# One plan for the orders of all engines in the second stage of a four-layer GNN kernel, and Strassen's scheme for one LSTM step

## The chip, the cores and the metric

The kernel runs on one core of a Trainium2 chip, in one launch, all in fp32. The metric is the device time of a run in microseconds (us). TensorE is called PE, VectorE DVE, ScalarE ACT, GpSimd POOL, and SyncE, which issues DMAs, SP.

## What is computed

The input x has 128 graphs of 64 nodes with 256 features; all share one 64 x 64 adjacency matrix. Four layers follow, each `x = layernorm(x + layer(x))`:

```
layer 0   three graph convolutions with adj * adj: 256 -> 512 -> 1024 -> 256, relu after the first two
layer 1   eigenvectors U of the normalised Laplacian: U (relu(U^T x W1 + b1) W2 + b2)
layer 2   two graph convolutions with adj (256 -> 256), then, for p = 1, 2, 3, 4:
          an LSTM of p steps over each window of p nodes; its last hidden state replaces the window's last node
layer 3   h = x W + b; softmax over nodes of (h h^T * adj), times h
```

One LSTM step has eight units of 128 outputs, four gates (i, f, g, o) in two halves of the hidden size:

```python
g = x_t @ Wih.T + h @ Whh.T + bias
i, f, gg, o = jnp.split(g, 4, axis=-1)
c = sigmoid(f) * c + sigmoid(i) * tanh(gg)
h = sigmoid(o) * tanh(c)
```

## The kernel before

**Tiles and stages.** The 8192 rows are 64 tiles of 128 rows (two graphs), taken as 16 groups of four tiles. All rows lie in SBUF in X for the whole run. The first stage does layer 0 for all groups (`layer0`, L744), its middle product already by Strassen's scheme (L777 to L840), while `eigen` finds U on DVE in small steps in between. The norms of the first stage are ACT and POOL steps kept in a list, `norms`; each product of `layer0` takes one off (L832). What is left of the list is done in the second stage. Layers 1 to 3 are the second stage: `group` (L1187) is a generator through `layer1`, `layer2` with `lstm`, and `layer3`.

**Matmuls.** `mm` (L715) issues one matmul and moves a planner's clock, `now`. Nearly all matmuls of the kernel are put down to its line 716; transposes go through `turn` (L925, line 926).

**LSTM.** `hT` holds the group's features on partitions, 64 nodes x 8 graphs on the free axis. `lstm(hT, p, first, nw)` (L991) runs p steps over nw windows, so matmuls have n = 8 nw columns: 256 for p = 1 and 2, 168 for p = 3, 128 for p = 4. In a step t > 0, each of the eight units has four matmuls into one PSUM bank, two with `wih` (from x) and two with `whh` (from h, L1029), then a tanh on ACT with the bias from PSUM (L1030). Sigmoids are taken as tanh of half the argument. DVE then forms c (L1034 to L1038), ACT its tanh (L1039), DVE the new h (L1041, or L1051 into `hT`). The first two units' `wih` matmuls go ahead of the wait for h (L1008).

**What sets the order.** PE's order in the second stage is written out by hand, under `manual_schedule` for PE alone (L1205). Three groups (WAYS) are under way. A generator yields the time at which its next step may start: the clock plus a fixed allowance (MOVE, MIXED, LIN, CONV, NORM, SOFT and CELL, L922 and L923, 1.2 to 5.2 us). The loop takes the oldest group whose time has come (L1214); once no group is left to start, the one with the fewest steps done, with LEAD = 10 steps of advance for each older group. DVE, ACT and POOL aren't under `manual_schedule`: the framework orders their instructions, with two copies given priority (L952, L1122). The last two groups (ENDING) do layer 3 in two halves and their last norms on ACT.

**Engines and waits.** Every engine takes its instructions in order and waits on semaphores. A group's step passes from PE through PSUM (eight banks) to ACT or DVE and back to PE.

Of the kernel before, what the change touches and what calls it, by code (L numbers as in the profile page):

```python
# [1 line left out]

# [8 lines left out]
F32 = mybir.dt.float32  # L11
# [4 lines left out]
N = 64  # L16
# [24 lines left out]
class Timed:  # L41
# [6 lines left out]
    def __getattr__(self, name):  # L48
        def give(out, *args, **kw):
            self.free[0] = max(self.free[0], self.until[0]) + self.least + 0.0009 * max(0, np.prod(out.shape[1:]) - 64)  # L50
            return getattr(self.engine, name)(out, *args, **kw)  # L51

        return give

# [484 lines left out]
LEAD = 10  # L539
# [57 lines left out]
def kernel(  # L597
# [51 lines left out]
    X = keep.tile([P, NT, D], F32, name="X")  # L649
# [4 lines left out]
    nc.scalar.dma_start(X[:, 2:4, :], x_t[:, 2:4, :])  # L654
    for t in range(2):
        nc.sync.dma_start(X[:, t, :], x_t[:, t, :])
# [6 lines left out]
    for t in range(4, NT, 2):  # L663
        nc.sync.dma_start(X[:, t:t + 2, :], x_t[:, t:t + 2, :])
# [79 lines left out]
    def layer0(g):  # L744
        xs = X[:, 4 * g:4 * g + 4, :]
# [108 lines left out]
        for t in (2, 0):  # L854
            p = tl(psa, [P, 2, D], "ps", bufs=6)
            mm(p, sqT2, s3[:, t:t + 2, :])
            yield now[0]
            x2 = xs[:, t:t + 2, :]
            VL.tensor_add(x2, p, x2)
            norms.extend(scalar_norm(tc, small, x2, half, spare))  # L860

# [45 lines left out]
    pg = ctx.enter_context(tc.tile_pool(name="pg", bufs=WAYS, reuse_waits="tile"))  # L907
    pw = ctx.enter_context(tc.tile_pool(name="pw", bufs=5, reuse_waits="tile"))
    pv = ctx.enter_context(tc.tile_pool(name="pv", bufs=4, reuse_waits="tile"))
    psb = ctx.enter_context(tc.tile_pool(name="psb", bufs=8, space=bass.MemoryType.PSUM, reuse_waits="tile"))  # L910
# [10 lines left out]
    now[0] = due[0] = 0.0  # L921
    MOVE, MIXED, LIN, CONV, NORM, SOFT = 1.2, 1.2, 1.5, 1.8, 5.2, 5.2  # L922
    CELL = {256: 3.8, 168: 2.2, 128: 1.9}  # L923

    def turn(out, in_):  # L925
        PE.transpose(out, in_, ident)  # L926
        now[0] += 0.11

    def work():
        return tl(pw, [P, 1024], "w")  # L930

    def work2():
        return tl(pv, [P, 512], "v")

    spare[0] = lambda: work2()[:, :D]

    def ps4(shape=(P, 512)):
        return tl(psb, list(shape), "ps")
# [4 lines left out]
    def mixed(src, rhs, ready):  # L943
# [3 lines left out]
        for t in range(4):  # L947
            if t % 2 == 0:
                yield ready[t // 2]
            for c in range(2):  # L950
                mm(ps[c][:, t * P:(t + 1) * P], src[:, t, c * P:(c + 1) * P], rhs)
        with tc.high_priority(offset=1500):  # L952
            V.tensor_copy(dst[:, 0, :], ps[0])
        S.copy(dst[:, 1, :], ps[1])
        yield now[0] + MIXED
        return dst

    def norm(xs, t, ready, more=0.0, scalar=False):
        rows_norm(tc, small, xs[:, t:t + 2, :], half, scalar)
        ready.append(now[0] + NORM + more + (0.8 if ready else 0.0))  # L960

    def layer1(xs, ready):
        a = yield from mixed(xs, u2, ready)
        for t in range(0, 4, 2):
            V.tensor_add(xs[:, t:t + 2, :], xs[:, t:t + 2, :], ub2.unsqueeze(1).to_broadcast([P, 2, D]))
        h = as3(work2(), 4)
        for t in range(0, 4, 2):
# [5 lines left out]
            yield now[0]  # L973
        yield now[0] + LIN
        z = work2()
        p = ps4((P, 4, P))
        for t in range(4):
            mm(p[:, t, :], h[:, t, :], ut2)
        S.copy(as3(z, 4), p)
        yield now[0] + MOVE  # L980
        ready = []
        for t in range(0, 4, 2):
            p = ps4((P, 2, D))
            for j in range(2):
                mm(p[:, j, :], z[:, (t + j) * P:(t + j + 1) * P], bw2)
            V.tensor_add(xs[:, t:t + 2, :], p, xs[:, t:t + 2, :])  # L986
            norm(xs, t, ready, 2.0)
            yield now[0]
        return ready

    def lstm(hT, p, first, nw):  # L991
# [6 lines left out]
        for t in range(p):  # L998
# [4 lines left out]
            G = tl(pg, [P, 2048], "gates")[:, :2 * len(names) * n].rearrange("p (q h n) -> p q h n", h=2, n=n)  # L1003
            gate = {q: G[:, i] for i, q in enumerate(names)}
            units = [(h, q) for h in range(2) for q in names]

            ahead = {}
            early = units[:2] if t else []  # L1008
            for h, q in early:
                m = slice(("ifgo".index(q) * 2 + h) * P, ("ifgo".index(q) * 2 + h + 1) * P)  # L1010
                ahead[h, q] = pp = ps4()[:, :n]
                for k in range(2):
                    mm(pp, wi[:, k, m], xt[k], k == 0, False)
            if t:
                yield ready
            if p > 1 and not t:
                c = tl(pg, [P, 512], "c")[:, :2 * n].rearrange("p (h n) -> p h n", h=2)
            new = None if last else tl(pg, [P, 512], "hs")[:, :2 * n].rearrange("p (h n) -> p h n", h=2)
            for h, q in units:
                j = 2 * "ifgo".index(q) + h  # L1020
                m = slice(j * P, (j + 1) * P)
                pp = ahead.get((h, q))
                if pp is None:
                    pp = ps4()[:, :n]
                    for k in range(2):
                        mm(pp, wi[:, k, m], xt[k], k == 0, k == 1 and not t)
                if t:
                    for k in range(2):
                        mm(pp, wh[:, k, m], hs[:, k, :], False, k == 1)  # L1029
                S.activation(gate[q][:, h, :], pp, AF.Tanh, bias=bias[:, j:j + 1], scale=0.5 if q == "g" else 0.25)  # L1030
                if q == "g":
                    to = gate["g"][:, h, :] if t or p == 1 else c[:, h, :]
                    if t:
                        V.scalar_tensor_tensor(c[:, h, :], gate["f"][:, h, :], 1.0, c[:, h, :], op0=ALU.add,  # L1034
                                               op1=ALU.mult)
                    V.scalar_tensor_tensor(to, gate["i"][:, h, :], 1.0, gate["g"][:, h, :], op0=ALU.add, op1=ALU.mult)  # L1036
                    if t:
                        V.scalar_tensor_tensor(c[:, h, :], c[:, h, :], 0.5, to, op0=ALU.mult, op1=ALU.add)  # L1038
                    S.activation(gate["i"][:, h, :], c[:, h, :] if p > 1 else to, AF.Tanh, scale=0.5)  # L1039
                if q == "o" and not last:  # L1040
                    V.scalar_tensor_tensor(new[:, h, :], gate["o"][:, h, :], 1.0, gate["i"][:, h, :], op0=ALU.add,  # L1041
                                           op1=ALU.mult)
                if q == "o":
                    if h == 0:
                        yield now[0]
                elif h == 1 or len(units) == 8:
                    yield now[0]
# [7 lines left out]
            ready = now[0] + CELL[n]  # L1055
            hs = new
        return ready

    def layer2(xs, g, ready):
        a = yield from mixed(xs, adT2, ready)  # L1060
        g1 = as3(work(), 4)
        ready = []
        for t in range(0, 4, 2):
            p = ps4((P, 2, D))
            for j in range(2):
                run(p[:, j, :], [(a[:, k, (t + j) * P:(t + j + 1) * P], cw0[:, k, :]) for k in range(2)])
            V.tensor_add(g1[:, t:t + 2, :], p, wide["c_b0"].unsqueeze(1).to_broadcast([P, 2, D]))
            relu(g1[:, t:t + 2, :], g1[:, t:t + 2, :])
            ready.append(now[0] + CONV)
            yield now[0]  # L1070
        a = yield from mixed(g1, adT2, ready)
        hT = tl(pw, [P, 1024], "w").rearrange("p (k n b) -> p k n b", k=2, b=8)
        for c in range(2):
            p = ps4((P, 4, P))
            run(p, [(cw1[:, k, c * P:(c + 1) * P], a[:, k, :]) for k in range(2)])
            h = work2()
            V.scalar_tensor_tensor(as3(h, 4), rs_row.unsqueeze(1).to_broadcast([P, 4, P]), cb1[:, c:c + 1], p,
                                   op0=ALU.mult, op1=ALU.add)
            S.activation(hT[:, c, :, :].rearrange("p n b -> p b n"), as3(h, 8), AF.Relu, scale=2.0)
            yield now[0]  # L1080
        ready = now[0] + CONV
        for p, first, nw in ((1, 0, 32), (1, 32, 32), (2, 0, 32), (3, 0, 21), (4, 0, 16)):
            if first == 0:
                yield ready
            ready = yield from lstm(hT, p, first, nw)
        hb = as3(work(), 2)
        V.tensor_copy(as3(hb[:, 0, :], 8), hT[:, 0, :, :].rearrange("p n b -> p b n"))
        S.copy(as3(hb[:, 1, :], 8), hT[:, 1, :, :].rearrange("p n b -> p b n"))
        yield ready + 1.6
        ready = []  # L1090
        for t in range(0, 4, 2):
            p = ps4((P, 2, D))
# [169 lines left out]
```

## Time and profile before

| | us |
|---|---|
| median of 3 runs (2534.43 to 2536.97) | 2536.52 |
| the profiled execution | 2540.87 |
| its span, first to last instruction | 2539.1 |
| PE busy | 2494.8 |
| DVE busy | 1407.8 |
| ACT busy | 1090.6 |
| POOL busy | 134.2 |

The profile is of one execution, whose own time is 2540.87 us, 1.8 us more than its span. An engine's busy time is the time in which at least one of its instructions was under way. Matmuls overlap one another and their ends are modelled. PEld is the loading of weights, which overlaps matmuls. A row of the windows view has a stretch and its length in us, then the busy us of PE, PEld, DVE, ACT and POOL with instructions in brackets, the granted PE clock as a share of full speed, the DMA share and GB/s. A row of the waits view has the waiting engine, what it wrote and the line, then what released it: us in total, times, longest. A row of the timeline has start, us from the first start to the last end, engine, line, operation, output<-inputs, shapes and how many in a row.

### The profile page before, as it was taken

The numbers are of one execution on the slowest core, as the hardware profiler recorded it, in microseconds if no ns is written. First come the engines' busy times: TensorE is split into PE (matmuls) and PEld (weight loads), VectorE is DVE, ScalarE is ACT, GpSimd is POOL, SyncE is SP. The second block draws the span as 40 slices with busy tenths as digits, with TensorE's granted clock in tenths as the row PEclk, the third lists the DMA queues.
The fourth block names the chain that finished last, engine by engine and source line by source line (L and its number), as shares of the span: only waits on it lengthen the run. The fifth ranks groups of instructions, "written<-read, shape, count | busy, mean of one in ns | idle before, by whom it ended". The sixth has DMA issues, their size and how long they took to land.

```text
span 2539.1 us, 39015 instructions
## 1 busy us (share of the span) xinstructions
PE 2494.8 (98%) x15020; PEld 2196.2 (86%) x15020; DVE 1407.8 (55%) x4996; ACT 1090.6 (43%) x2706; POOL 134.2 (5%) x316
## 2 busy tenths in 40 slices
PE   9999999999999999999999999999999999999997
PEld 7788887888878889998989889898998998978996
DVE  6888777778885433454453543544445345353235
ACT  2344333433333344445344444444444534535454
POOL 0000000000000100000000000000000000010001
PEclk9999999999999999999999999999999999999998
DMA  6000000000000300000000000000000000000000
GB/s 219 1 1 1 1 1 1 1 1 1 1 1 1 117 1 1 10 9 1 9 9 1 9 1 10 9 1 9 1 9 9 1 9 9 1 9 1 1 1 26
DMA packets 24634, 32.09 MB, mean 13 GB/s; under 512 B 2176, under 2 KB 21376, under 8 KB 24448
## 3 DMA queue, kind: packets, MB, share of 16 engines
q1 hardware_dynamic: 24096, 29.32, 3.4%
q8 instruction: 118, 1.93, 0.3%
q14 instruction: 68, 0.56, 0.1%
q10 hardware_dynamic: 352, 0.28, 0.0%
HBM read 21.20 MB, written 8.39 MB: 12 GB/s over the span
## 4 chain that ended last, share of the span: by engine, by line
PE 91%; DVE 5%; POOL 2%; issue 1%; DMA 0%; ACT 0%; SPq 0%; ACTq 0%; POOLq 0%; DVEq 0%
PE ps L716 88%; PE ps L926 2%; POOL ln_rs L554 1%; DVE X L564 1%; DVE ln_st L551 1%; DVE D L51 1%; PE ps L1146 1%; PE pc L93 1%; DMA X<-in_x_dram 0%; POOL ln_rs L553 0%; DVE tw L51 0%; DVE ln_mv L552 0%; DVE X L1176 0%; DVE X L986 0%; DVE X L1096 0%
## 5 line engine op out<-in xcount | busy, mean ns | idle before, releaser
L716 PE MATMUL ps<-w,wih 128*128 128x256 f32 (+2 forms) x4992 | 894.0, 319 | 1.8 <-DVE w L1051 1.8
L716 PEld LDWEIGHTS ps<-w,wih 128*128 128x128 f32 x4992 | 760.9, 191 | 47.8 <-issue 5.7
L1030 ACT ACTIVATE gates<-ps,cbi 128x128 f32<-128x128 f32 (+2 forms) x1248 | 499.3, 410 | 523.3 <-PE ps L716 516.2
L716 PE MATMUL ps<-hs,whh 128*128 128x128 f32 (+2 forms) x3072 | 540.5, 303 | 6.2 <-DVE hs L1041 6.2
L716 PEld LDWEIGHTS ps<-hs,whh 128*128 128x128 f32 x3072 | 453.9, 191 | 32.9 <-issue 11.2
L1036 DVE SCALAR_TENSOR_TENSOR gates<-gates 128x256 f32<-128x256 f32 (+2 forms) x256 | 89.3, 349 | 297.4 <-ACT gates L1030 297.4
L716 PE MATMUL ps<-aw,h 128*128 128x256 f32 x1024 | 227.2, 379 | 0.0
L716 PEld LDWEIGHTS ps<-aw,h 128*128 128x128 f32 x1024 | 192.9, 190 | 25.9 <-ACT h L725 0.5
L725 ACT ACTIVATE h<-h 128x512 f32<-128x512 f32 x128 | 80.5, 629 | 170.0 <-DVE h L51 169.8
L1039 ACT ACTIVATE gates<-c 128x128 f32<-128x128 f32 (+2 forms) x288 | 98.1, 341 | 114.1 <-DVE c L1038 87.9
L1034 DVE SCALAR_TENSOR_TENSOR c<-gates,c 128x128 f32<-128x128 f32 (+2 forms) x192 | 62.6, 326 | 139.4 <-ACT gates L1030 138.2
L1051 DVE SCALAR_TENSOR_TENSOR w<-gates 128x256 f32<-128x256 f32 (+2 forms) x160 | 59.6, 376 | 108.5 <-PE ps L716 73.5
L716 PE MATMUL ps<-ss,tw 128*128 128x256 f32 x512 | 117.9, 380 | 0.0
L716 PE MATMUL ps<-ss,aw 128*128 128x256 f32 x512 | 117.3, 379 | 0.0
L716 PE MATMUL ps<-m,aw 128*128 128x256 f32 x512 | 117.1, 380 | 0.0
L716 PE MATMUL ps<-aw,m 128*128 128x512 f32 x256 | 114.8, 594 | 0.0
L1041 DVE SCALAR_TENSOR_TENSOR hs<-gates 128x128 f32<-128x128 f32 (+2 forms) x192 | 62.6, 326 | 93.6 <-ACT gates L1039 52.4
L553 POOL TENSOR_SCALAR ln_rs<-ln_mv 128x2 f32<-128x2 f32 x96 | 26.2, 273 | 1558.4 <-DVE ln_mv L552 1557.9
L716 PEld LDWEIGHTS ps<-ss,aw 128*128 128x128 f32 x512 | 96.6, 190 | 12.8
L716 PEld LDWEIGHTS ps<-ss,tw 128*128 128x128 f32 x512 | 96.3, 190 | 12.9 <-issue 0.2
L564 DVE TENSOR_SCALAR X<-X,ln_mv,ln_rs 128x256 f32<-128x256 f32 x176 | 64.7, 410 | 75.9 <-POOL ln_rs L554 75.9
L716 PEld LDWEIGHTS ps<-m,aw 128*128 128x128 f32 x512 | 95.6, 190 | 12.6 <-issue 0.5
(294 smaller groups left out, 3107.4 us busy)
## 6 DMA issues: line engine op xcount, KB each, us to landing
X<-in_x_dram SPq DMA_DIRECT2D x30, 256.0 KB, 6.3
out_dram<-X SPq DMA_DIRECT2D x28, 256.0 KB, 2.1
wih<-in_c_ih_dram SPq DMA_DIRECT2D x4, 1024.0 KB, 7.2
aw<-in_a_w_dram SPq DMA_DIRECT2D x3, 1024.0 KB, 10.3
whh<-in_c_hh_dram SPq DMA_DIRECT2D x3, 1024.0 KB, 9.4
out_dram<-X SPq DMA_DIRECT2D x8, 128.0 KB, 1.7
aw<-in_a_w_dram SPq DMA_DIRECT2D x1, 512.0 KB, 5.8
cw<-in_c_w_dram SPq DMA_DIRECT2D x2, 256.0 KB, 5.1
```

The source lines that it names most:

```text
L51: return getattr(self.engine, name)(out, *args, **kw)
L553: nc.gpsimd.tensor_scalar(rs, mv[:, :, 1], EPS, None, op0=ALU.add)
L564: nc.vector.tensor_scalar(x[:, t, :], x[:, t, :], mv[:, t, 0:1], rs[:, t:t + 1], op0=ALU.subtract, op1=ALU.mult)
L716: PE.matmul(out, lhsT, rhs, start=start, stop=stop)
L725: S.activation(dst, src, AF.Relu)
L926: PE.transpose(out, in_, ident)
L1030: S.activation(gate[q][:, h, :], pp, AF.Tanh, bias=bias[:, j:j + 1], scale=0.5 if q == "g" else 0.25)
L1034: V.scalar_tensor_tensor(c[:, h, :], gate["f"][:, h, :], 1.0, c[:, h, :], op0=ALU.add, op1=ALU.mult)
L1036: V.scalar_tensor_tensor(to, gate["i"][:, h, :], 1.0, gate["g"][:, h, :], op0=ALU.add, op1=ALU.mult)
L1039: S.activation(gate["i"][:, h, :], c[:, h, :] if p > 1 else to, AF.Tanh, scale=0.5)
L1041: V.scalar_tensor_tensor(new[:, h, :], gate["o"][:, h, :], 1.0, gate["i"][:, h, :], op0=ALU.add, op1=ALU.mult)
L1051: V.scalar_tensor_tensor(hT[:, h, slice(first + p - 1, first + nw * p, p), :], gate["o"][:, h, :].rearrange("p (w b) -> p w b", b=8), 1.0, ...
```

## The change

**A plan.** Five classes are new. The functions of the second stage no longer issue anything. They describe each step to a `Plan` as an `Op` with an engine, calls, and a cost. The plan finds dependencies from the parts of tiles that steps read and write, and keeps a time for every engine and every buffer slot. Over and over it takes, of all engines, the step that can start first; among steps of an engine that can start within 0.02 us of one another it takes the oldest group's, or for PE, once no group is left to start, that of the group with the most steps left. A step of another engine is ready at its predecessor's end and the predecessor's LAG; a step of the same engine right at the end. `manual_schedule` covers PE, DVE, ACT and POOL now. The allowances, the generators and LEAD are gone. `products` notes matmuls, `turns` transposes.

**Strassen for p = 2, t = 1.** `second` takes the place of the eight units for the second step of row pairs. The 256 x 256 blocks of the weights are combined once (`add_weights`: four sums of 512 columns for each of `wih` and `whh`). The windows are cut into two halves of 16, the features into two blocks; four sums of each of x and h are formed on DVE (128 columns each). Seven products replace eight, each of matmuls of 128 columns with x and h adding up in PSUM. DVE and one ACT copy a half combine them in SBUF; tanh then reads SBUF.

**Rows set aside.** The weight sums take 16 KB of a partition. X keeps 44 tiles. Layer 0 takes groups 11 to 15 first; each is stored to DRAM after its norm, and rows of groups 0 to 4 are loaded in its place. In the second stage, when group g < 5 is done, the rows of group 11 + g come back.

**Smaller edits.** In `layer1` the matmuls with `ut2` are noted in two pairs, each after its half of the relu. In `layer3` the scores and softmax come ahead of the transposes for `hn`. `hb` is copied in halves. Stores of the output are one tile each. The left-over norms of the first stage are noted as steps, 1.5 us apart.

```diff
+class Plan:
+    LAG = {"PE": 0.20, "DVE": 0.118, "ACT": 0.137, "POOL": 0.04, "SP": 2.0}
...
+    def run(self, groups, ways):
+        going, todo = {}, list(enumerate(groups))
+        able = {e: [] for e in self.engines}
+
+        def rank(op):
+            if op.engine == "PE" and not todo:
+                return -going[op.group]
+            return op.group or 99
+
+        while todo or going:
+            while todo and len(going) < ways + (0 in going):
...
+            best = None
+            for e, ops in able.items():
+                first = []
+                for op in ops:
+                    t = max(self.free[e], op.ready)
+                    for tile in op.tiles:
+                        if tile.real is None and tile.slot is None:
+                            t = max(t, min(self.slots[tile.tag]))
+                    if t < 1e9:
+                        first.append((t, op))
+                if first:
+                    t0 = min(t for t, _ in first)
+                    t, op = min((x for x in first if x[0] <= t0 + 0.02), key=lambda x: (rank(x[1]), x[1].rank))
+                    if best is None or t < best[0]:
+                        best = t, op
...
+            self.emit(op)
+            op.start = t
+            self.free[e] = t + op.cost
+            end = t + op.cost + self.LAG[e]
...
+            for other in op.after:
+                other.ready = max(other.ready, t + op.cost if other.engine == e else end)
...
+            if cost is None and self.engine == "DVE":
+                cost = {"bn_aggr": 0.082, "reciprocal": 0.095}.get(name, 0.067 + n / 960)
+                if name == "tensor_scalar" and not any(isinstance(x, Part) for x in args[2:]):
+                    cost = 0.067 + n / 1920
+            elif cost is None and self.engine == "ACT":
+                cost = (0.145 if bank else 0.110) + n * 0.00083
...
-    X = keep.tile([P, NT, D], F32, name="X")
+    X = keep.tile([P, NT - 4 * LATE, D], F32, name="X")
+    aside = ctx.enter_context(tc.tile_pool(name="aside", bufs=1, space=bass.MemoryType.DRAM))
+    rest = [aside.tile([P, 4, D], F32, name=f"rest{i}") for i in range(LATE)]
+    order = list(range(NT // 4 - LATE, NT // 4)) + list(range(NT // 4 - LATE))
...
+        def change():
+            nc.sync.dma_start(rest[g], xs)
+            for t in (0, 2):
+                nc.sync.dma_start(xs[:, t:t + 2, :], given(order[g + LATE])[:, t:t + 2, :])
...
+    def add_weights():
+        for w, s in zip((wih[1], whh[1]), sums):
+            a11, a12, a21, a22 = quarters(w)
+            V.tensor_add(s[:, 0], a21, a22, ready=30.0)
+            V.tensor_sub(s[:, 1], s[:, 0], a11, ready=30.0)
+            V.tensor_sub(s[:, 2], a11, a21, ready=30.0)
+            V.tensor_sub(s[:, 3], a12, s[:, 1], ready=30.0)
+
+    def products(calls):
+        cost = sum(2 * max(0.00084 * int(np.prod(c[2].shape[1:])) if not isinstance(c[2], Part) else 0.00084 * c[2].at.size,
+                           0.112) for c in calls)
+        plan.note("PE", [("matmul", (o, l, r), {"start": a, "stop": z}) for o, l, r, a, z in calls], cost)
...
+    def turns(pairs):
+        plan.note("PE", [("transpose", (out, in_, ident), {}) for out, in_ in pairs], 0.218 * len(pairs))
...
+    def second(hT, xt, hs, G, c, bias):
...
+        for s, b1, b2 in ((0, x1, x2), (1, h1, h2)):
+            V.tensor_sub(T1[s], b1[1], b1[0])
+            V.tensor_sub(T2[s], b2[1], T1[s])
+            V.tensor_sub(T3[s], b2[1], b1[1])
+            V.tensor_sub(T4[s], b2[0], T2[s])
+        moving = ((x1[0], h1[0]), (x2[0], h2[0]), (x2[1], h2[1]), T4, T1, T2, T3)
+        weight = (0, 1, 6, 2, 3, 4, 5)
+        for h in range(2):
+            u1 = work2()[:, :256].rearrange("p (q n) -> p q n", q=2)
+            a, b, c12, d = (G[:, h, w, m] for w in range(2) for m in range(2))
+
+            def two(*which):
+                p = ps4((P, 2, 2, P))
+                for at, i in enumerate(which):
+                    for q in range(2):
+                        run(p[:, at, q, :], [(ways[s][weight[i]][:, q, h, :], moving[i][s]) for s in range(2)])
+                return p[:, 0], p[:, 1]
+
+            p1, p2 = two(0, 1)
+            S.copy(u1, p1)
+            V.tensor_add(a, u1, p2)
+            p6, p7 = two(5, 6)
+            V.tensor_add(c12, u1, p6)
+            V.tensor_add(b, c12, p7)
+            p5, p3 = two(4, 2)
+            V.tensor_add(d, b, p5)
+            V.tensor_add(c12, c12, p5)
+            V.tensor_add(c12, c12, p3)
+            p4, _ = two(3)
+            V.tensor_add(b, b, p4)
+            gate = {}
+            for m, q, name in ((0, 0, "i"), (0, 1, "g"), (1, 0, "f"), (1, 1, "o")):
+                j = 2 * "ifgo".index(name) + h
+                gate[name] = G[:, h, :, m, q, :]
+                S.activation(gate[name], gate[name], AF.Tanh, bias=bias[:, j:j + 1],
+                             scale=0.5 if name == "g" else 0.25)
+            ch = c[:, h, :].rearrange("p (w n) -> p w n", w=2)
+            V.scalar_tensor_tensor(gate["g"], gate["i"], 1.0, gate["g"], op0=ALU.add, op1=ALU.mult)
+            V.scalar_tensor_tensor(ch, gate["f"], 1.0, ch, op0=ALU.add, op1=ALU.mult)
+            V.scalar_tensor_tensor(ch, ch, 0.5, gate["g"], op0=ALU.mult, op1=ALU.add)
+            S.activation(gate["i"], ch, AF.Tanh, scale=0.5)
+        for h in range(2):
+            for w in range(2):
+                o, i = (G[:, h, w, m, 0 if m == 0 else 1, :].rearrange("p (w b) -> p w b", b=8) for m in (1, 0))
+                V.scalar_tensor_tensor(hT[:, h, 32 * w + 1:32 * w + 32:2, :], o, 1.0, i, op0=ALU.add, op1=ALU.mult)
...
+    with tc.manual_schedule(engines={mybir.EngineType.PE, mybir.EngineType.DVE, mybir.EngineType.Activation,
+                                     mybir.EngineType.Pool}):
+        plan.run([left_over] + [lambda g=g: group(g) for g in range(NT // 4)], WAYS)
```

## The prediction, made before the result

> **What bounds the kernel now.** I read the page first: how much each engine is busy, and which engine the chain that ended last runs through.
>
> ```profile
> span 2539.1 us, 39015 instructions
> PE 2494.8 (98%) x15020; PEld 2196.2 (86%) x15020; DVE 1407.8 (55%) x4996; ACT 1090.6 (43%) x2706; POOL 134.2 (5%) x316
> ...
> PE 91%; DVE 5%; POOL 2%; issue 1%; DMA 0%; ACT 0%; SPq 0%; ACTq 0%; POOLq 0%; DVEq 0%
> ```
>
> TensorE (PE) is busy 98% and carries 91% of the chain; no other engine is near full. Time comes off in two ways only: less matmul time, or less PE idling. The windows view (busy us by stage, then the granted clock) says where PE idles. The second stage begins near 868 us.
>
> ```profile
> 868.00:900.00 32.00, 27.87 (x158) 23.87 (x157) 19.62 (x54) 10.17 (x25) 6.61 (x15) 0.89 0.17 66
> 900.00:2240.00 1340.00, 1328.07 (x8880) 1211.43 (x8880) 601.46 (x1699) 620.11 (x1543) 71.07 (x144) 1.00 0.02 6
> 2240.00:2280.00 40.00, 34.25 (x201) 30.59 (x198) 24.11 (x67) 10.77 (x23) 5.03 (x10) 0.87 0.04 14
> 2280.00:2460.00 180.00, 180.00 (x1189) 169.47 (x1188) 57.01 (x163) 91.00 (x232) 0.92 (x2) 1.00 0.00 1
> 2460.00:2539.10 79.10, 62.25 (x478) 53.86 (x476) 43.54 (x150) 35.62 (x91) 14.46 (x40) 0.87 0.06 21
> ```
>
> PE idles 4.1, 11.9, 5.8, 0 and 16.9 us. Where the clock column is under 1, busy time is stretched too: 0.11 x 32 = 3.5 us and 0.13 x 40 = 5.2 us. So start, middle and the place at 2240 lose 7.6 + 11.9 + 11.0 = 30.5 us, and the end at least 16.9. The waits view of PE in 900 to 2460 names what it waited for:
>
> ```profile
> PE ps L716 <- DVE X L564: 6.9, 5, 2.8
> PE ps L716 <- DVE hs L1041: 5.4, 4, 1.3
> PE ps L716 <- ACT v L725: 3.0, 1, 3.0
> ```
>
> These are hand-overs (a norm, an LSTM cell, a relu) that came later than PE's hand-written order supposed. The timeline gives the pace of matmuls. A matmul of the program appears as two records and a transpose as one.
>
> ```profile
> 1499.65 4.70 PE L716 MATMUL ps<-w,wih 128*128 128x256 f32 x21
> ...
> 2460.87 1.04 PE L926 MATMUL ps<-ident,w 128*128 128x128 f32 x8
> ...
> 2462.64 1.50 PE L716 MATMUL ps<-w,wih 128*128 128x128 f32 x12
> ...
> 2481.87 0.42 DVE L1150 TENSOR_TENSOR v<-ps,adst 128x256 f32<-128x256 f32 x1
> ...
> 2482.32 0.29 DVE L1151 TENSOR_SCALAR v<-v 128x256 f32<-128x256 f32 x1
> ...
> 2482.65 0.43 DVE L1152 TENSOR_TENSOR v<-v 128x256 f32<-128x256 f32 x1
> ```
>
> A 256-column record has a mean of 380 ns, but they overlap: (4.70 - 0.38)/20 = 0.216 us from start to start. A 128-column one (275 ns): (1.50 - 0.275)/11 = 0.111. A transpose (273 ns): (1.04 - 0.273)/7 = 0.110. Those paces, not the means, are the price on PE.
>
> **What the Trainium skill says.** "TensorE: Matmul & The Clock Gate", section "What's actually happening": after an idle window of about 3.4 us PE falls to half clock until it has been busy again. The trace agrees in kind: the clock is 0.87 just where PE waited 2.8 and 3.0 us within 8 us, and 1.00 in the 1340 us whose stalls are at most 1.7 us; so long stalls cost double. The same page, "Step-by-step": matmuls stay in program order, only weight loads are pulled ahead. So one late operand stops all groups' matmuls behind it, as the 2.8 us wait shows. "VectorE: DVE Perf Modes", section on the errata: an fp32 tensor_tensor lasts (N+151)/0.96 ns, 424 ns at 256 columns and 291 at 128; the trace has 414 (L971, PSUM source) and 284 (L1152): agreed.
>
> **The change part by part**, against the profiled execution's 2540.9 us; the shown median, 2536.5, is 4.4 lower, and I carry each gain over to it unchanged.
>
> *Strassen, PE.* Step two of the row pairs now costs 8 units x 4 matmuls = 32 matmuls of 256 columns, 64 records x 0.216 = 13.8 us a group. Seven products x 2 gate pairs x 2 halves x 2 sources = 56 matmuls of 128 columns, 112 records x 0.1116 = 12.5 us (0.1116 is the mean over all such starts of the stage). Gain 1.3 a group, **-21 us** in 16. Strided 128-column operands already run at this pace in steps of row quadruples (L1013 with n = 128), so I give it no penalty.
>
> *Strassen, other engines.* DVE gains 8 subtractions of 128 columns (8 x 0.284 = 2.3), 14 combinations of 256 columns with a PSUM source (14 x 0.414 = 5.8), and four writes of hT of 128 instead of two of 256 (4 x 0.291 - 2 x 0.419 = 0.3): +8.4 us a group. In the middle window DVE is busy 601/1340 = 45%, 46 of 102.8 us a group (the pattern of the chain repeats after 205.5 us, two groups). It becomes 54 of 101, 54%. ACT gains two PSUM copies (2 x 0.383) and eight tanh from SBUF in place of PSUM (412 for 472 ns): +0.3 on 47. Neither becomes the bound, so I cost both at nothing; the other two groups' matmuls hide them. Without that cover the second step's tail alone (two adds of 0.414, four tanh of 0.412, three DVE steps of 0.419, tanh, write) is 4.6 us, 73 us in all. The copies ahead of the transposes come in halves: the same elements, 0.
>
> *Weight sums.* Eight operations of 512 columns, 8 x 0.68 = 5.5 us of DVE once, set at 30 us of the stage. DVE is 61% busy in 868 to 900, and the last weights land at 875.0, so the fixed order doesn't wait for them: 0, at most +3.
>
> *All orders fixed.* PE's order becomes greedy: what can start first by the plan, the oldest group first. It has no margins, where the allowances of L922 and L923 had some. Two errors decide. First, a DVE step that needs the one before it starts later than the plan's cost says: 0.45 and 0.33 us above against 0.334 and 0.200 in the plan, 0.12 each; a cell has up to two such pairs, so I take a hand-over to be 0.2 us late. Second, a transpose is planned at 0.218 and takes 0.110, so a bundle of four ends 0.44 us early and covers less. A late hand-over costs nothing where PE is in another group's bundle; a bundle is some 8 records of 0.11, 0.88 us, so a lateness d costs d x d / (2 x 0.88) on average: 0.023 us for 0.2, and 0.11 for 0.44. I count 25 hand-overs a group (mixes, relus, copies, norms, softmax, ten cell steps): 25 x 16 x 0.023 = 9 us. Seven transpose bundles, half of them ahead of a waiting step: 3.5 x 16 x 0.11 = 6. The start, where all groups are equally young, keeps 4 of its 7.6. Sum 19 instead of 30.5: **-11**; bounds: 4 (-26) and 36 (+6).
>
> *The end.* With the most remaining steps first, the last three groups end together. Their third layers overlap, but share DVE: the last norm, row store and softmax still follow each other. Of 16.9 idle us I take off 4: **-4**; bounds -12 and +8.
>
> *Rows set aside.* Twenty tiles go to DRAM and back: 5 x 0.5 MB each way, on SP, which waits for a norm before each store; behind it stand only the next loads, needed several groups (868/16 = 54 us each) later. An input load of 256 KB lands in 6.3 us. 0. Each changed group leaves one entry more in the list of norms than its products take off, so some five more ACT norms come after the stage's start, on an engine that is 32% busy there: 0. The output goes out tile by tile, so SP issues four stores a group for two; only the rows' loads stand behind them: 0. POOL's order is fixed too; it is 5% busy, and the plan's 0.78 us for its power step is above the 0.71 it takes: 0.
>
> Sum: 2540.9 - 21 - 11 - 4 = 2504.9 profiled; for the median **2500**.
>
> **The rivals.**
> (a) The stalls stay as they are, at other places; only Strassen pays: 2536.5 - 21 = 2515. For it: both errors named above, dependent DVE steps and transposes, leave PE too little cover. Against: one account of every engine sees the contention that fixed due times can't.
> (b) The plan is nearly exact: start and middle lose 4, the end 12 less: 2536.5 - 21 - 26 - 12 = 2477. For it: no PE idling in 180 us with three groups at hand. Against: the errors above.
> (c) Slower: fixed FIFO orders without margin. When a DVE or ACT step waits for an operand, ready steps of the other two groups stand behind it, and PE waits for those in turn, so lateness adds up. With lateness d the stalls are 400 x d x d / 1.76; they eat all 51 us (30.5 + 21, less 4 of the start, plus 4 of the end) at d = 0.47 us. At 0.6 they are 82: 2536.5 + 82 - 51 = 2567. For it: DVE gets 18% more work in long dependent chains just here. Against: DVE to PE, 0.31 us for a 128-column step at 2466.2, is the plan's 0.32.
>
> **How the numbers follow.** Forecast 2500 (2488 to 2512): 0.50. (a), with somewhat more stalls: 2512 to 2531: 0.22. (b): 2470 to 2488: 0.16. (c): 0.10. Within 0.2% (5 us, about what a measurement of this kernel can tell from no change): 0.02 beside, and 0.02 from the edge of (a). So faster 0.86, same 0.04, slower 0.10. The range 2476 to 2526 leaves out (c), the low quarter of (b) and the edge of (a).
>
> **What would show it.** PE's records rise by 768 and its busy time falls by some 20 us; the new matmuls start every 0.112 us; windows of steady groups repeat after some 101 us; no clock under 1 between 900 and the end; DVE at 54%. I am wrong if the new matmuls start slower than 0.123 us (then Strassen gains nothing), if PE idles over 1.5% of the middle, or if DVE's own waits for PE grow and PE's waits name DVE.

## The result, and the profile after

The changed kernel takes **2590.69 us** (median of 4 runs) against 2535.52 us before on the same chip: a ratio of **1.022, 95% interval 1.0202 to 1.0237, slower**. The prediction was 2500 us and faster. Its profiled execution has a span of 2591.6 us, 52.5 more than before. First the page of the changed kernel: totals, and the shares of the chain that ended last.

```profile
span 2591.6 us, 41095 instructions
PE 2501.8 (97%) x15788; PEld 2200.0 (85%) x15788; DVE 1551.3 (60%) x5404; ACT 1103.1 (43%) x2754; POOL 139.2 (5%) x316
...
PE 85%; DVE 11%; ACT 3%; issue 1%; POOL 0%; DMA 0%; SPq 0%; ACTq 0%; POOLq 0%; DVEq 0%
```

PE has its 768 new records, but carries only 85% of the chain; DVE and ACT now own 14% of it. Work has been put *between* matmuls. The windows view says where, in the stretches used before:

```profile
868.00:900.00 32.00, 31.58 (x185) 27.15 (x185) 24.00 (x56) 20.23 (x46) 6.52 (x14) 1.00 0.15 59
900.00:2240.00 1340.00, 1280.99 (x9129) 1165.36 (x9129) 692.43 (x1973) 597.97 (x1501) 69.90 (x144) 1.00 0.02 8
2240.00:2280.00 40.00, 38.16 (x284) 31.90 (x284) 21.49 (x58) 18.12 (x41) 1.85 (x4) 1.00 0.00 1
2280.00:2460.00 180.00, 176.49 (x1149) 163.70 (x1149) 87.08 (x244) 84.95 (x206) 5.65 (x12) 1.00 0.01 4
2460.00:2591.60 131.60, 112.58 (x920) 103.65 (x918) 64.43 (x211) 62.83 (x172) 15.23 (x40) 0.93 0.04 13
```

PE idles 0.4 us at the start instead of 4.1, but **59.0 us in the middle instead of 11.9**. The waits view of PE, 900 to 2400 us, names the releasers (total us, times, longest):

```profile
PE ps L151 <- DVE gates L151: 22.1, 42, 1.1
PE ps L151 <- ACT v L151: 16.5, 19, 1.1
PE ps L151 <- DVE w L151: 9.2, 9, 2.1
PE ps L151 <- ACT w L151: 5.5, 14, 0.5
PE ps L151 <- ACT att L151: 4.7, 13, 0.4
```

Line 151 is the plan's `emit`, through which every step goes, so tiles tell the waits apart. `gates` written by DVE is a Strassen combination, and most of `v` written by ACT is `u1`, the copy of the first product. But PE doesn't read either of them: why does it wait? The timeline of the second step of one group (weight loads and other rows left out):

```profile
1869.80 1.50 PE L151 MATMUL ps<-w,sums 128*128 128x128 f32 x12
...
1871.34 0.42 DVE L151 TENSOR_TENSOR gates<-v,ps 128x256 f32<-128x256 f32 x1 [0.85 <-PE ps L151]
...
1871.82 0.94 PE L151 MATMUL ps<-w,sums 128*128 128x128 f32 x6 [0.51 <-DVE gates L151]
...
1874.70 1.71 ACT L151 ACTIVATE gates<-gates,cbi 128x256 f32<-128x256 f32 x4 [6.11 <-DVE gates L151]
...
1876.31 0.35 ACT L151 COPY v<-ps 128x256 f32<-128x256 f32 x1
...
1876.71 0.49 PE L151 MATMUL ps<-w,wih 128*128 128x128 f32 x2 [1.06 <-ACT v L151]
```

The twelve records are product p6 and half of p7, at (1.50 - 0.275)/11 = 0.111 us, as predicted. Then PE stops until DVE has added p6 (1871.34 to 1871.76), and only then does the second half of p7. In `two`, p6 and p7 share one PSUM bank, in different columns. At 1876.71 it is the copy of p1, itself behind four tanh in ACT's order, that holds up the second half of p2. The views take releasers from semaphores, so these matmuls wait on a semaphore of DVE or ACT; the plan, which compares columns, knows nothing of it. The half of p7 that comes before the reader in program order ran without a wait. The Trainium skill ("PSUM — Partial Sum Buffer", section "The four PSUM rules") says that the compiler back end, for XLA's own matmuls, puts any two engines' accesses to one bank and quadrant (32 partitions) in order. These matmuls are not XLA's, but they fill all 128 partitions, and the trace shows the same order kept: four such waits in this group, 0.68 to 1.22 us from start to start above the pace each. What put the waits into the program isn't shown.

There is a second kind of stall, here once every two groups, from the same view:

```profile
1960.56 0.46 ACT L151 ACTIVATE gates<-ps,cbi 128x256 f32<-128x256 f32 x1
...
1961.32 0.88 DVE L151 SCALAR_TENSOR_TENSOR X<-ps,sm,X 128x256 f32<-128x256 f32 x2 [0.46 <-PE ps L151]
...
1963.32 0.60 PE L151 MATMUL ps<-w,wih 128*128 128x256 f32 x2
...
1963.95 0.42 DVE L151 BATCH_NORM_STATS2 st<-X 128x6 f32<-128x256 f32 x1
1964.40 0.18 DVE L151 BATCH_NORM_AGGREGATE mv<-st 128x2 f32<-128x6 f32 x1
...
1965.45 0.17 DVE L151 BATCH_NORM_AGGREGATE mv<-st 128x2 f32<-128x6 f32 x1
1965.54 0.39 DVE L151 SCALAR_TENSOR_TENSOR w<-gates 128x256 f32<-128x256 f32 x1
...
1965.99 3.29 PE L151 MATMUL ps<-w,wih 128*128 128x256 f32 x14 [2.07 <-DVE w L151]
```

PE waits for one write of `hT` (1965.54), whose operands ACT had finished by 1961.02. It stands behind 14 DVE steps of an older group's residual and norm, which the plan put first. An aggregate starts 0.45 us after the statistics it needs; the plan allows 0.334. But such errors make only a part of this stall: from 1961.32 to the write are 4.22 us, and the same 14 steps cost 3.67 us by the plan's own formulas. So 0.55 us are lateness. Most of the 2.2 us that PE loses here (start to start, above the pace) is the plan's own doing: its times, worked out from the kernel, leave PE 1.79 us without a step at this place.

### The profile page after: what moved, and what is told of

Its sections match the earlier page's. It is cut to its first block, busy times and chain, and to the rows that moved or that the text cites. A ratio compares the mean times of both kernels' runs of the same rounds, so it can differ in the third digit from the quotient of the medians.

```text
span 2591.6 us, 41095 instructions
## 1 busy us (share of the span) xinstructions
PE 2501.8 (97%) x15788; PEld 2200.0 (85%) x15788; DVE 1551.3 (60%) x5404; ACT 1103.1 (43%) x2754; POOL 139.2 (5%) x316
## 4 chain that ended last, share of the span: by engine, by line
PE 85%; DVE 11%; ACT 3%; issue 1%; POOL 0%; DMA 0%; SPq 0%; ACTq 0%; POOLq 0%; DVEq 0%
PE ps L151 54%; PE ps L915 30%; DVE X L151 2%; DVE gates L151 2%; ACT gates L151 2%; DVE st L151 2%; DVE v L151 1%; DVE D L52 1%; DVE w L151 1%; DVE mv L151 1%; PE pc L276 1%; ACT w L151 1%; DVE tw L52 0%; POOL rs L151 0%; ACT v L151 0%
## 5 line engine op out<-in xcount | busy, mean ns | idle before, releaser
L151 PE MATMUL ps<-w,wih 128*128 128x128 f32 (+2 forms) x4864 | 848.7, 311 | 26.3 <-ACT v L151 14.4
L151 PEld LDWEIGHTS ps<-w,wih 128*128 128x128 f32 x4864 | 728.4, 192 | 68.8 <-ACT v L151 17.2
L151 ACT ACTIVATE gates<-ps,cbi 128x128 f32<-128x128 f32 (+2 forms) x1120 | 440.5, 401 | 380.9 <-PE ps L151 367.3
L151 PE MATMUL ps<-hs,whh 128*128 128x128 f32 (+1 forms) x2816 | 460.9, 287 | 1.1 <-DVE hs L151 0.8
L151 PEld LDWEIGHTS ps<-hs,whh 128*128 128x128 f32 x2816 | 395.4, 192 | 3.8 <-DVE hs L151 2.5
L151 PE MATMUL ps<-w,sums 128*128 128x128 f32 x896 | 123.2, 281 | 22.3 <-DVE gates L151 22.1
L151 PEld LDWEIGHTS ps<-w,sums 128*128 128x128 f32 x896 | 109.3, 192 | 31.0 <-DVE gates L151 30.7
L151 ACT ACTIVATE gates<-gates,cbi 128x256 f32<-128x256 f32 x128 | 54.9, 497 | 174.6 <-DVE gates L151 174.5
L151 POOL TENSOR_SCALAR rs<-mv 128x2 f32<-128x2 f32 x96 | 23.5, 245 | 1632.4 <-DVE mv L151 1630.9
```

The costliest lines, as they stand in the source:

```text
L151: getattr(e, name)(*[real(x) for x in args], **{k: real(v) for k, v in kw.items()})
```

## The experiments

**Theory B**: products that share a PSUM bank make PE wait for the readers of each other. **Theory D** (my rival (c)): in-order queues without margin pile up lateness, wherever it comes from. In what follows, the plan's *account* is its table of costs and lags. Ratios are to the kernel before on the same chip.

**x1: a bank for each product.**

```diff
-                p = ps4((P, 2, 2, P))
-                for at, i in enumerate(which):
+                out = []
+                for i in which:
+                    p = ps4((P, 2, P))
                     for q in range(2):
-                        run(p[:, at, q, :], ...)
-                return p[:, 0], p[:, 1]
+                        run(p[:, q, :], ...)
+                    out.append(p)
+                return out
...
-            p4, _ = two(3)
+            p4, = two(3)
```

> Each of Strassen's seven products gets a PSUM bank of its own instead of two sharing one; nothing else changes. Theory B (a product's matmuls wait for DVE or ACT to have read the other product in the same bank, which the plan doesn't know): the four waits of 0.68 to 1.22 us in every group's second step go, 3.26 us a group, 52 us in all: about 2539 us. Theory D (in-order queues without margin add up lateness everywhere, the bank is only where it shows): the waits move to other hand-overs, 2575 to 2591 us.

2538.87 us, ratio 1.0005 (0.9996 to 1.0013): 52 us less than the changed kernel, B's number. Its waits of PE, 900 to 2400 us:

```profile
PE ps L151 <- DVE w L151: 9.8, 10, 2.1
PE ps L151 <- ACT w L151: 5.4, 13, 0.5
PE ps L151 <- ACT att L151: 4.7, 13, 0.4
PE ps L151 <- DVE X L151: 3.4, 8, 0.6
PE ps L151 <- ACT v L151: 1.7, 3, 0.8
```

The 22.1 us on `gates` are gone and `v` is down from 16.5 to 1.7; the other rows have hardly moved. The plan's order and times are the same in both kernels, so only the PSUM banks differ: the bank waits were a loss of their own.

**x2: banks shared, but known to the plan.**

```diff
-                mask[x.at.reshape(-1)] = True
+                mask[slice(None) if t.tag == "ps" else x.at.reshape(-1)] = True
```

> Banks shared as in the changed kernel, but the plan takes any two steps on one PSUM bank as dependent, so it plans a read of a bank after all matmuls into it. Theory B: PE no longer waits inside a bank; each combination comes a product (0.9 us) later: 2539 to 2555 us. Theory D: 2575 to 2595 us.

2533.5 us, ratio 0.9984 (0.9977 to 0.999), just below B's range. (The edit covers every PSUM tile of the second stage, not only Strassen's.) So sharing a bank needn't be slow: what costs is an order that lets a reader in between two products of one bank.

**x3: the plan without Strassen** (`PAIRS = False`).

> The plan alone: the second step of row pairs as eight units of four matmuls again, no weight sums, rows still set aside. Theory B: 52 us of bank waits go and 21 us of matmul time come back, 2590.7 - 52 + 21 = 2560 us, and PE's other stalls (some 4 us a group) stay. Theory D: Strassen's waits are part of a general lateness that stays: 2591 to 2612 us. My prediction's view, that the plan by itself saves 11 to 15 us of stalls: 2521 us.

2552.36 us, ratio 1.0059 (1.0042 to 1.0075). Nearest to B's 2560 and far from my 2521: the plan without Strassen (with the rows set aside and the smaller edits) is 0.6% *slower* than the hand-written order. Something besides the banks is wrong with it.

**x4: the plan's account corrected**, banks still shared.

```diff
-                other.ready = max(other.ready, t + op.cost if other.engine == e else end)
+                other.ready = max(other.ready, t + op.cost + (0.12 if e == "DVE" else 0.0) if other.engine == e else end)
...
-        plan.note("PE", [("transpose", (out, in_, ident), {}) for out, in_ in pairs], 0.218 * len(pairs))
+        plan.note("PE", [("transpose", (out, in_, ident), {}) for out, in_ in pairs], 0.11 * len(pairs))
```

> Only the plan's account changes: a DVE step that needs the DVE step before it is ready 0.12 us later, and a transpose costs 0.11 instead of 0.218 us. Theory B: only the stalls outside the second step shrink, of about 4.3 us a group perhaps half, so 2555 to 2580 us, and the bank waits stay. Theory D: with the account right most stalls go, below 2545 us.

2529.67 us, ratio 0.9967 (0.9955 to 0.9978): 61 us less, D's number, and too much for B alone. What is left of PE's waits:

```profile
PE ps L151 <- DVE gates L151: 26.0, 41, 0.9
PE ps L151 <- DVE w L151: 1.5, 2, 1.1
PE ps L151 <- ACT v L151: 1.1, 2, 0.8
PE ps L151 <- ACT w L151: 0.8, 5, 0.2
```

Now it is the bank wait that stays and all the others that go: the mirror image of x1. (The one on `v` went too, since in the new order the copy no longer falls between its two products.) B holds for the banks. Of D it is shown that the account's errors cost as much again, but not that this lateness piles up along a queue.

**x5: both repairs.**

> Both repairs: a bank for each product, and the corrected account (0.12 us between dependent DVE steps, 0.11 for a transpose). If bank waits and wrong account are two separate losses, their gains add: 2590.7 - 52 - 61 = 2478 us, up to 2495 if some stalls only move. If they are one loss seen twice (lateness that either repair absorbs): 2520 to 2535 us.

**2488.11 us, ratio 0.9807 (0.9793 to 0.9822): below both kernels**, 1.9% under the one before, and near the sum of the two gains. By the plan x5 has x4's order and times, so the 42 us between these two are the banks'. The middle of its span, and PE's waits in 900 to 2400:

```profile
900.00:2240.00 1340.00, 1337.49 (x9695) 1236.46 (x9694) 723.97 (x2109) 641.51 (x1584) 81.99 (x160) 1.00 0.03 8
```

```profile
PE ps L151 <- DVE w L151: 1.2, 2, 0.8
PE ps L151 <- ACT w L151: 0.8, 5, 0.2
PE ps L151 <- DVE hs L151: 0.5, 1, 0.5
```

PE idles 2.5 us in 1340.

**x6: the corrected plan without Strassen** (`PAIRS = False` in x5).

> The corrected account with the second step as eight units again, so the plan alone. If Strassen brings its 21 us of matmul time once nothing stalls: 21 us above the run with both repairs, about 2500 us. If its DVE work and longer chain cost part of it: less than 12 us above.

2521.07 us, ratio 0.9938 (0.9923 to 0.9953). A right plan, with the rows set aside and the smaller edits, gains some 16 us; which of these it comes from wasn't tried. Strassen brings 33 us on top, more than its 21 of matmul time and outside both expectations: x6 idles 8.3 us in the middle where x5 idles 2.5, and more at its end. That these extra 12 us belong to Strassen, and not to how the two plans happen to fall, isn't shown.

**x7 and x8: the two halves of the correction alone**, in the changed kernel: the 0.12 us between dependent DVE steps, then the transposes' 0.11.

> Of the account only the 0.12 us between dependent DVE steps; transposes stay at 0.218, banks stay shared. If late DVE steps are what the account's 61 us come from: 2532 to 2545 us. If the transposes are: above 2570 us.

> Of the account only the transpose at 0.11 us; DVE steps stay as in the changed kernel, banks stay shared. If DVE's lateness is the cause: 2575 to 2592 us. If the early transposes are: 2532 to 2560 us.

2563.45 us (1.0108, 1.0091 to 1.0124) and 2573.58 us (1.0144, 1.0129 to 1.0159): 27 and 17 us less than the changed kernel. Neither expectation fits (x8 only just misses 2575): no single error makes up the 61 us, DVE's is the larger, and together they bring 17 us more than their sum. One row tells them apart: PE's waits on `att`, the softmax, stay with only DVE's repair (5.7 us, 13 times, in x7) and are gone from the view with only the transposes' (x8). The wait on `w` doesn't go with either: 6.9 us in x7, 5.8 in x8, 1.5 with both.

**x9: the order of DVE, ACT and POOL left to the framework**, PE's by the plan, with both repairs (`manual_schedule` for PE alone, on x5).

> Both repairs, but the plan's order binds PE alone; DVE, ACT and POOL are ordered by the framework as before the change. If the fixed order of the other engines is where lateness spreads (my rival of FIFO orders without margin): as fast or faster than 2488 us. If one account for all engines needs the others to keep to it: slower, 2500 us or more.

2503.4 us, ratio 0.9861 (0.9844 to 0.9877), 15 us slower than x5. With a right account, fixed orders on the other engines are a gain over leaving them free under a PE order that counts on them. With the wrong account this wasn't tried, so rival (c) is answered for the right account alone.

**x10: as x4, with the banks known to the plan as in x2.**

> Banks shared, with the corrected account and with the plan taking steps on one bank as dependent. If sharing costs only because the plan doesn't know of it: close to the run with a bank each, 2485 to 2495 us. If sharing itself slows matmuls or reads: above 2505 us.

2507.24 us, ratio 0.9876 (0.9861 to 0.9891): by the number the second expectation, 19 us above x5. But its reason isn't seen: no wait is left in the second step, and the matmuls keep their paces. Instead PE loses 0.84 and 0.91 us a group in layer 1, where it waits for ACT's copy into `v` and DVE's into `w` (8.1 and 9.0 us in the waits view). Why this plan ends with these two isn't settled; a bank for each product is the better repair.

PE's idle time between 900 and 2240 us, from the windows view of each kernel:

| | wrong account | right account |
|---|---|---|
| two products in a bank | 59.0 (changed kernel, 2590.7) | 27.0 (x4, 2529.7) |
| a bank for each | 26.7 (x1, 2538.9) | 2.5 (x5, 2488.1) |

## Why the prediction was wrong

Adding up the distances between matmul starts splits the 52.5 us. At their paces (0.1117 us for 128 columns, 0.1426, 0.2159, 0.4292 for 168, 256, 512, 0.0375 for 64, 0.109 for a transpose) all matmuls take 2466.7 us before and 2445.8 after: **-20.9, as predicted**. All that lies above those paces grows from 61 to 134 us: +73. One of the prediction's own signs of being wrong came true: PE idles 4.4% of the middle (59.0 of 1340 us), not at most 1.5%.

- *Strassen, PE*: right in size, pace and records. "I give it no penalty" was said of the pace of strided operands, and held (0.111 us).
- *Strassen, other engines*: DVE's busy time rose by 143.5 us against 8.4 x 16 + 5.5 = 140, and stood at 692.43/1340 = 52% in the middle, against 54. The volumes were right. **The first step that failed is "so I cost both at nothing; the other two groups' matmuls hide them".** I priced the 56 matmuls and the DVE steps apart and never asked what the new buffer ties together. Two products share a bank, with readers of one in between the matmuls of the other; this is in the diff (`p[:, 0], p[:, 1]`). A matmul that waits for such a reader holds up the other groups' matmuls too, so they hide nothing. It costs 52 us (changed kernel to x1). No rival of mine had it.
- *All orders fixed, -11*: **the second step that failed.** With *the end*, -4, the plan should have saved 15 us; without Strassen it cost 15 (x3), and with Strassen and a bank each it ate the 21 us (x1), both beyond my bounds of +6 and +8. Both errors of the plan were named with their right sizes, 0.12 us a dependent DVE pair and 0.11 a transpose, but the formula, 9 + 6 us from independent hand-overs, undersized them: repairing both took off 61 us (shared banks), 51 (a bank each) or 31 (no Strassen, x3 to x6). Nor do they add as independent charges: 27 and 17 alone, 61 together. By what path they cost so much is open in part. Lateness that adds up behind another group's steps, rival (c)'s mechanism, makes some 0.5 us of the one long stall taken apart above. The prediction has no term for the idle time that the plan's own order puts there, 1.79 us.
- *The start* kept 0.4 us, not 4. *The end*: 16.9 us of idling became 19.0, where I had taken off 4.
- *Rows set aside, weight sums*: 0 holds as far as shown. By 868 us PE has 4129 records behind it before and 4128 after. The rows' return in the second stage and the sums were never tried alone.
- Rival (c) had the sign, and gave 2567. Its mechanism is shown only in part, and fixed orders as such aren't the harm once the account is right (x9). Rival (a), stalls kept and only Strassen paying, gave 2515; with the banks repaired, x1 has 2539, so the stalls are larger than before.
- That x5 comes within 12 us of the forecast of 2500 is partly luck: its matmul time is the forecast's, but its time above the paces is 37 us less than before, where I took off 15.

## What to carry to other kernels

When several results share a PSUM bank and are read one by one, ask for each matmul which reader of that bank comes before it in program order: here it waited for that reader, whatever columns they used. A static order for all engines is worth as much as its account: check each cost, and above all the gap between two dependent steps of one engine, against a trace before trusting it; here two errors of 0.11 and 0.12 us cost 61 us of 2591. Don't price such errors one by one, as independent: together they cost more here than their sum. And read the plan's own idle times before blaming lateness: a greedy order can plan a stall.

## What the runs showed of the hardware that was not expected

A stall of 2.2 us can be followed by half clock. In the changed kernel the same stall (2.07 us in the waits view, 2.2 from start to start above the pace) comes three times, at 1747, 1964 and 2178 us. After two of them the windows view has the clock at 0.72 over 6 us (some 3.4 us at half), after the other at 1.00:

```profile
1749.00:1755.00 6.00, 5.43 (x17) 4.48 (x18) 3.66 (x13) 2.75 (x7) 1.03 (x2) 0.72 0.27 90
1965.00:1971.00 6.00, 5.01 (x24) 4.46 (x25) 4.40 (x15) 3.15 (x8) 1.03 (x2) 1.00 0.26 87
2180.00:2186.00 6.00, 5.28 (x17) 4.43 (x18) 3.47 (x12) 2.65 (x7) 1.03 (x2) 0.72 0.27 90
```

The Trainium skill ("TensorE: Matmul & The Clock Gate", section "What's actually happening") speaks of an idle window of about 3.4 us that runs freely; here a shorter stall was enough twice. It costs little: some 1.7 us each time, an estimate from 0.28 x 6. The prediction's sign "no clock under 1 between 900 and the end" thus failed, but it isn't what made the kernel slower.
